# A graph network kernel: one gathered column in seven of layer 1 comes from one-hot products on TensorE

## The chip, the cores and the metric

The kernel runs on one core of a Trainium2 chip. The metric is the device time of one execution in microseconds. Five engines of the core appear in the text: TensorE (PE, with its weight loads shown apart as PEld), VectorE (DVE), ScalarE (ACT), GpSimd (POOL) and SyncE (SP). Each works through its own instructions in the order of the program and waits for others by semaphores.

## The reference

There are 12,500 nodes with 32 features and 400,000 edges `src -> dst`, sorted by `dst`. Three graph-attention layers (two of 2 heads with 16 channels, one of 1 head with 32) are followed by a residual layer norm, an edge network with a maximum over each node's edges, and a second residual layer norm. A layer is:

```python
h = (x @ W.T).reshape(n, heads, ch)
a_s = (h * att_s[None]).sum(-1); a_d = (h * att_d[None]).sum(-1)
logits = leaky_relu(a_s[src] + a_d[dst], slope)
m = segment_max(logits, dst)
ex = exp(logits - m[dst]); denom = segment_sum(ex, dst)
alpha = ex / (denom[dst] + 1e-16)
out = segment_sum(alpha[:, :, None] * h[src], dst) + bias
```

After layers 1 and 2 come an ELU and a clip to [-3, 3]. The edge network is `relu([x[src], x[dst], edge_attr] @ W1 + b1) @ W2 + b2`, of which each node takes the maximum over its edges.

## The kernel before

The sorted edges lie in 128 rows of TE = 3125, one row per partition, so that an edge column t holds one edge of each partition. The 12,500 nodes, padded to 12,544, lie as 128 partitions x NC = 98.

Preparation (up to 303 us): the node table of layer 1 (`tb`, 36 values per node: 32 features, two source logits, and the places of the node's last and first edge) is computed on TensorE and written to `table1` in DRAM. The first edge of each node is found with 98 gathers (`found`). The destination logits are scattered (`give`). `empties` fills the rows for nodes without edges in all tables, through SP's transfers.

Each of the three layers (`attention(li, idx)`) then walks over 54 chunks of the columns: 50 of T = 60, and four of 48, 32, 29 and 16. For each column one indirect DMA on POOL (`gather`, line 68) fetches 128 rows of the node table into a tile `g`; the index is `src` in layer 1, and the place of the source node's last or first edge (`src_last`, `src_first`, taken out of the gathered rows at L683 and L684) in layers 2 and 3 and in the edge network. `g` has four buffers. With a chunk's rows there, DVE and ACT work out the logits (`lg`), running maxima (`mx`) and running sums by scans along the row (`gf`, L723 multiplies, L734 scans). `finish` divides by the sums (L494 to L501), applies the ELU, and in four sub-blocks of up to 16 columns adds, transposes and multiplies with the next layer's weights (`yb` L523, `yt` L525, `ph` L528, `pa` L529, `tb` L531, `at` L532). SP writes `sums`, `table` and `give` to DRAM.

The program is recorded in source order and a scheduler then places the instructions of each engine; the work of neighbouring chunks is interleaved on DVE, PE and ACT. Each engine executes its list strictly in that order. At the end of a layer POOL scatters 49 columns of `x0` (`move`), gathers one row of `sums`, and scatters the rows of the partitions' ends, after which the next layer's gathers begin.

The edge network has the same chunks and gathers `xs` by `src_last` (four buffers). It transposes three inputs per sub-block (`xt` L870, `et` L871, `xst` L872), multiplies them with two halves of the first weights (L877) and the second weights (L883), takes the maximum by scans (L887) and normalises (`layernorm`, L540 to L548).

PSUM tiles: `small_p` is a tile of each layer's pool; the biases lie in a tile `fixed`.

Of the kernel before, what the change touches and what calls it, by code (L numbers as in the profile page):

```python
# [24 lines left out]
def gnn_resnorm_kernel(ctx: ExitStack, tc: tile.TileContext, a: dict, out: bass.AP):  # L25

# [56 lines left out]

    groups = [(c0, min(28, NC - c0)) for c0 in range(0, NC, 28)]
# [19 lines left out]
    gpool = gstack.enter_context(tc.tile_pool(name="g", bufs=4, side="right"))  # L104
# [4 lines left out]
    x0 = runs.tile([P, NC, D], F32, name="x0")  # L109
# [22 lines left out]
    fixed = ctx.enter_context(tc.tile_pool(name="fixed", bufs=1, space=PSUM)).tile([P, 512], F32, name="fixed")  # L132
    own = const.tile([P, 1], F32, name="own")
    nc.gpsimd.iota(own, pattern=[[1, 1]], base=E + NN, channel_multiplier=1,
                   allow_small_or_imprecise_dtypes=True)
    zeros = const.tile([P, 1250], F32, name="zeros")
# [59 lines left out]

    table1 = dram.tile([NN, D + 4], F32, name="table1")
# [10 lines left out]
    def clear(table, part=0, parts=1):  # L208
        flat = edge_rows(table).rearrange("p t w -> p (t w)")
        k = TE * table.shape[1] // parts  # L210
        z = next(z for z in range(1250, 0, -1) if k % z == 0)
        tc.keep_in_program_order(
            nc.sync.dma_start(out=flat[:, part * k:part * k + k].rearrange("p (k z) -> p k z", z=z),
                              in_=bcast(zeros[:, None, :z], [P, k // z, z])))
# [83 lines left out]
    cont = runs2.tile([P, TE + 1], F32, name="cont")  # L298
    src_last = runs2.tile([P, TE], I32, name="src_last")
# [14 lines left out]
    with tc.tile_pool(name="seg", bufs=1) as sp, tc.tile_pool(name="rowsp", bufs=2) as rp, \  # L314
# [52 lines left out]
        for c0, n in groups:  # L367
            rows = rp.tile([P, 28, SB], I32, name="found")
            for c in range(n):
                gather(rows[:, c, :], dst_d, find_i[:, c0 + c:c0 + c + 1])  # L370
            less = rp.tile([P, 28, SB], BF16, name="less")[:, :n, :]
            nc.vector.tensor_tensor(less, rows[:, :n, :], bcast(node_p[:, c0:c0 + n, None], [P, n, SB]), op=ALU.is_lt)
            nc.vector.tensor_reduce(r[:, c0:c0 + n], less, axis=AX.X, op=ALU.add)
            nc.vector.tensor_add(first[:, c0:c0 + n], first[:, c0:c0 + n], r[:, c0:c0 + n])
# [15 lines left out]
        nc.sync.dma_start(out=node_rows(table1), in_=tb)  # L390

# [111 lines left out]
    def finish(li, pool, psum, den, v, n, hb=1):  # L503

        y = pool.tile([P, D * T], F32, name="y")[:, :D * n].rearrange("p (f t) -> p f t", t=n)
# [11 lines left out]
        for b in range(0, n, TB):  # L517
            nt = min(TB, n - b)
            w = nt * D
            pe = psum.tile([P, TB * D], F32, name="pe")[:, :w].rearrange("p (f t) -> p f t", t=nt)  # L520
            nc.scalar.activation(pe, e[:, :, b:b + nt], AF.Identity, bias=minus[:, 1:2])  # L521
            yb = pool.tile([P, TB * D], F32, name="yb", bufs=1)[:, :w].rearrange("p (f t) -> p f t", t=nt)
            nc.vector.scalar_tensor_tensor(yb, y[:, :, b:b + nt], 3.0, pe, op0=ALU.min, op1=ALU.add)  # L523
            yt = pool.tile([P, TB * D], F32, name="yt")[:, :w]
            nc.vector.transpose(blocks(yt), yb.rearrange("p f t -> p t f"))  # L525
            ph = psum.tile([P, TB * D], F32, name="ph", bufs=hb)[:, :w]
            pa = psum.tile([P, TB * D], F32, name="pa")[:, :w]
            nc.tensor.matmul(ph, lhsT=w_bd, rhs=yt, start=True, stop=True)  # L528
            nc.tensor.matmul(pa, lhsT=a_bd, rhs=yt, start=True, stop=True)  # L529
            at = pool.tile([P, TB, D], F32, name="at")[:, :nt, :]  # L530
            nc.vector.transpose(tb[:, b:b + nt, :D], blocks(ph))  # L531
            nc.vector.transpose(at, blocks(pa))  # L532
            nc.scalar.copy(tb[:, b:b + nt, D:], at[:, :, :heads])  # L533
            nc.scalar.copy(ta[:, b:b + nt, :], at[:, :, heads:2 * heads])
        return tb, ta

    def layernorm(lp, st, x, n):
        st = st[:, :n]
        sq = lp.tile([P, T, D], F32, name="sq", bufs=1)[:, :n, :]
# [10 lines left out]
    def finish3(pool, psum, den, v, x, n):  # L550
# [4 lines left out]
        layernorm(pool, den[:, 2 * T:], x, n)  # L555

    def empties():
# [4 lines left out]
        with tc.tile_pool(name="empty", bufs=2) as ep, tc.tile_pool(name="emptyps", bufs=1, space=PSUM) as eps:  # L562
# [66 lines left out]
    def attention(li, idx):  # L629
# [10 lines left out]
        with tc.tile_pool(name=f"s{li}", bufs=2) as sp, tc.tile_pool(name=f"f{li}", bufs=2) as fp:  # L640
# [18 lines left out]
            with tc.tile_pool(name=f"ps{li}", bufs=1, space=PSUM) as psp, \  # L659
                    tc.tile_pool(name=f"fps{li}", bufs=1, space=PSUM) as fps:  # L660

                small_p = psp.tile([P, 512], F32, name="small_p")
                den = small_p[:, 128:]
                old = None
                for c, (t0, n) in enumerate(todo):
                    g = gpool.tile([P, T * (D + 4)], F32, name="g")[:, :n * w].rearrange("p (t w) -> p t w", w=w)
                    for t in range(n):
                        gather(g[:, t, :], table, idx[:, t0 + t:t0 + t + 1])
# [44 lines left out]
                    rx = psp.tile([P, heads, 512], F32, name="rx", bufs=3 - heads)  # L713
# [5 lines left out]
                    for h in range(heads):  # L719
                        nc.scalar.activation(  # L720
                            rx[:, h, :FS * (n + 1)].rearrange("p (k t) -> p k t", t=n + 1),
                            bcast(rr[:, h:h + 1, :], [P, FS, n + 1]), AF.Exp)
                        nc.vector.tensor_mul(v[:, h * wd:h * wd + ch, cur].rearrange("p f t -> p t f"),  # L723
                                             g[:, :, h * ch:(h + 1) * ch], bcast(wt[:, h, :, None], [P, n, ch]))
                        nc.scalar.copy(v[:, h * wd + ch, cur], wt[:, h, :])  # L725
# [4 lines left out]
                    for h in range(heads):  # L730
                        for f in range(0, wd, FS):
                            k = min(FS, wd - f) * (n + 1)
                            o = (h * wd + f) * (n + 1)
                            nc.vector.tensor_tensor_scan(turned(gf[:, o:o + k], rev), turned(rx[:, h, :k], rev),  # L734
                                                         turned(gf[:, o:o + k], rev), 0.0, op0=ALU.mult, op1=ALU.add)
                    rows = sp.tile([P, T, gw + heads], F32, name="rows")[:, :n, :]
# [5 lines left out]
                    if li < 3:  # L742
                        tb, ta = finish(li, fp, fps, den, v[:, :, cur], n, hb=2)
# [61 lines left out]
    def edge_network(tag, in_order):  # L805


        with tc.tile_pool(name=f"in{tag}", bufs=2) as ip, tc.tile_pool(name=f"gx{tag}", bufs=4) as gp, \
                tc.tile_pool(name=f"v{tag}", bufs=2) as vp, tc.tile_pool(name=f"t{tag}", bufs=2) as tp, \
                tc.tile_pool(name=f"pf{tag}", bufs=1, space=PSUM) as pfp, \  # L810
                tc.tile_pool(name=f"ph{tag}", bufs=1, space=PSUM) as php:
            small_p = pfp.tile([P, 512], F32, name="small_p")
# [15 lines left out]

            old = None
            loaded = load(0)  # L830
            for c, (t0, n) in enumerate(todo):
                xs = gp.tile([P, T, D], F32, name="xs")
                for t in range(n):
                    gather(xs[:, t, :], tables[4], src_last[:, t0 + t:t0 + t + 1])
# [31 lines left out]
                for b in range(0, n, TB):  # L866
                    nt = min(TB, n - b)
                    w = nt * D
                    xt, et, st = (tp.tile([P, TB * D], F32, name=x)[:, :w] for x in ("xt", "et", "xst"))
# [29 lines left out]
                layernorm(tp, small_p[:, 128:], z, n)  # L899
# [58 lines left out]
```

## Time and profile before

| | us |
|---|---|
| median of the runs (3) | 18568.16 |
| lowest and highest | 18566.3, 18571.94 |
| profiled execution | 16382.21 |
| span of the profiled execution | 16379.3 |
| layer 1: first and last gather start | 303.2, 4249.9 |
| layer 2: first and last gather start | 4317.0, 8226.8 |
| layer 3: first and last gather start | 8294.0, 12202.3 |
| busy in the span: PE, DVE, ACT, POOL | 2781.3, 6836.7, 2899.1, 12218.7 |

The profiled execution is shorter than the runs shown; all durations below are from it. A row of the profile's groups names the line, the engine, the operation and its tiles, then the count, the busy time with the mean duration in nanoseconds, and the idle time of the engine before those instructions with what ended it. A row of the order in time gives the start and the duration in microseconds. "x2" merges two records that follow each other; an fp32 matmul leaves two records.

### The profile page before, as it was taken

The page shows a single profiled execution, that of the slowest core. Times are in us where ns is not written, and L with a number is a line of the kernel's source. Part 1 is how long each engine was busy: PE and PEld are TensorE (multiplying, and loading weights), DVE is VectorE, ACT ScalarE, POOL GpSimd, SP SyncE. Part 2 cuts the span into 40 slices and gives each one's busy share as a digit, 9 for nine tenths or more (in the row PEclk, how much of TensorE's full clock was granted, in tenths as well). Part 3 has the DMA queues.
Part 4 walks back from the last instruction along what each step waited for, and adds up shares of the span by engine and source line. Part 5 has one row for each costly group of instructions (what it writes and reads, how often), then busy time and mean ns, then how long its engine had stood idle before and what let it go on. Part 6 is the DMA issues. An engine that isn't in the chain of part 4 may idle for free.

```text
span 16379.3 us, 42394 instructions
## 1 busy us (share of the span) xinstructions
PE 2781.3 (17%) x5140; PEld 1116.2 (7%) x5140; DVE 6836.7 (42%) x9700; ACT 2899.1 (18%) x3835; POOL 12218.7 (75%) x12921
## 2 busy tenths in 40 slices
PE   0111111111111111111100000000003333334342
PEld 0000000000000000000000000000001111111110
DVE  2433333333333333333333333333335666666654
ACT  0221212121212222121211111111111111111111
POOL 6777777777777777777777777777767777777775
PEclk5555555555555555555555555555556666666676
DMA  4222222222222222222222222222222222222221
GB/s 59 71 60 69 60 55 73 55 48 42 43 41 47 41 44 44 43 45 41 46 47 58 51 56 53 56 53 55 54 57 59 66 66 64 66 66 64 69 63 42
DMA packets 580809, 897.63 MB, mean 55 GB/s; under 512 B 286271, under 2 KB 490238, under 8 KB 567070
## 3 DMA queue, kind: packets, MB, share of 16 engines
q0 software_dynamic: 413088, 226.62, 12.5%
q1 hardware_dynamic: 167116, 665.01, 11.5%
q10 hardware_dynamic: 304, 3.20, 0.1%
q14 instruction: 259, 2.11, 0.0%
q8 instruction: 42, 0.69, 0.0%
HBM read 390.67 MB, written 503.27 MB: 55 GB/s over the span
## 4 chain that ended last, share of the span: by engine, by line
POOL 71%; issue 23%; DMA 3%; DVE 1%; PE 0%; ACT 0%; POOLq 0%; DVEq 0%; ACTq 0%
POOL g L68 52%; POOL xs L68 17%; DMA g<-table,src_i 1%; DMA g<-table,src_last 1%; DMA xs<-table,src_last 1%; DMA g<-table,src_first 1%; POOL give L72 1%; POOL so L68 1%; POOL x_e L72 1%; PE ph L877 0%; DMA s<-sums,at_i 0%; PE pv L883 0%; DVE vf L887 0%; DVE z L803 0%; ACT xd L889 0%
## 5 line engine op out<-in xcount | busy, mean ns | idle before, releaser
L68 POOL DMA_INDIRECT g<-table,src_i x3125 | 2958.5, 947 | 989.6 <-issue 940.2
L68 POOL DMA_INDIRECT g<-table,src_last x3125 | 2957.1, 946 | 952.7 <-issue 938.1
L68 POOL DMA_INDIRECT xs<-table,src_last x3125 | 2954.9, 946 | 955.4 <-issue 936.8
L68 POOL DMA_INDIRECT g<-table,src_first x3125 | 2955.7, 946 | 952.7 <-issue 940.8
L697 DVE TENSOR_TENSOR lg<-g,af 128x60 f32<-128x60 f32 (+4 forms) x270 | 59.3, 250 | 4422.3 <-DMA g<-table,src_first 2333.3
L528 PE MATMUL ph<-yt,w_bd 128*128 128x512 f32 (+2 forms) x840 | 669.2, 893 | 3434.1 <-DVE yt L525 3434.1
L529 PE MATMUL pa<-yt,a_bd 128*128 128x512 f32 (+2 forms) x840 | 656.7, 878 | 3307.4 <-DVE at L532 3307.0
L877 PE MATMUL ph<-xt,wb_bd 128*128 128x512 f32 (+2 forms) x832 | 466.1, 645 | 2419.0 <-DVE xt L870 2419.0
L683 DVE CAST src_last<-g 128x60 int32<-128x60 f32 (+4 forms) x54 | 12.7, 235 | 2056.4 <-DMA g<-table,src_i 2056.4
L738 ACT COPY rows<-mx 128x120 f32<-128x120 f32 (+3 forms) x162 | 49.9, 308 | 4419.8 <-DVE mx L704 4366.5
L737 ACT COPY rows<-gf 128x2040 f32<-128x2040 f32 (+3 forms) x162 | 628.4, 3879 | 648.4 <-DVE gf L734 648.4
L734 DVE TENSOR_TENSOR_SCAN gf<-rx,gf 128x488 f32<-128x488 f32 (+4 forms) x918 | 731.9, 858 | 1.4 <-ACT gf L725 0.9
L591 PE MATMUL pt<-ident,tops 128*34 128x128 f32 (+1 forms) x3 | 1.0, 322 | 3954.6 <-DVE xr L548 3952.9
L723 DVE TENSOR_TENSOR gf<-g,small_p 128x960 f32<-128x960 f32 (+5 forms) x270 | 597.8, 2214 | 63.1 <-ACT small_p L715 63.1
L523 DVE SCALAR_TENSOR_TENSOR yb<-y,pe 128x512 f32<-128x512 f32 (+2 forms) x420 | 268.7, 640 | 605.2 <-ACT pe L521 586.7
L533 ACT COPY tb<-at 128x32 f32<-128x32 f32 (+4 forms) x420 | 92.3, 220 | 2333.8 <-DVE at L532 2333.8
L528 PEld LDWEIGHTS ph<-yt,w_bd 128*128 128x128 f32 x840 | 218.6, 287 | 3845.7 <-DVE yt L525 3367.3
L879 ACT ACTIVATE ht<-ph,b_c 128x512 f32<-128x512 f32 (+2 forms) x416 | 275.1, 661 | 1144.0 <-PE ph L877 1140.2
L529 PEld LDWEIGHTS pa<-yt,a_bd 128*128 128x128 f32 x840 | 220.3, 278 | 3681.9 <-DVE at L532 3511.5
L877 PE MATMUL ph<-et,wb_bd 128*128 128x512 f32 (+2 forms) x832 | 450.1, 626 | 0.0
L877 PE MATMUL ph<-xst,wb_bd 128*128 128x512 f32 (+2 forms) x832 | 431.2, 602 | 34.3 <-DVE xst L872 34.3
L883 PE MATMUL pv<-ht,w_bd 128*128 128x512 f32 (+2 forms) x832 | 415.3, 593 | 6.1 <-DVE vf L884 2.0
(295 smaller groups left out, 8591.8 us busy)
## 6 DMA issues: line engine op xcount, KB each, us to landing
sums<-rows SPq DMA_DIRECT2D x100, 1080.0 KB, 4.2
table<-tb SPq DMA_DIRECT2D x50, 1020.0 KB, 4.1
sums<-rows SPq DMA_DIRECT2D x50, 1020.0 KB
g<-table,src_i POOLq DMA_INDIRECT x3125
x_e<-zeros SPq DMA_DIRECT2D x10, 5000.0 KB, 16.8
g<-table,src_last POOLq DMA_INDIRECT x3125
g<-table,src_first POOLq DMA_INDIRECT x3125
xs<-table,src_last POOLq DMA_INDIRECT x3125
```

What stands on the lines that cost most here:

```text
L68: return nc.gpsimd.indirect_dma_start(out=dst, out_offset=None, in_=table, in_offset=bass.IndirectOffsetOnAxis(ap=idx, axis=0))
L72: return nc.gpsimd.indirect_dma_start(out=table, in_=src, in_offset=None, out_offset=bass.IndirectOffsetOnAxis(ap=idx, axis=0))
L523: nc.vector.scalar_tensor_tensor(yb, y[:, :, b:b + nt], 3.0, pe, op0=ALU.min, op1=ALU.add)
L528: nc.tensor.matmul(ph, lhsT=w_bd, rhs=yt, start=True, stop=True)
L529: nc.tensor.matmul(pa, lhsT=a_bd, rhs=yt, start=True, stop=True)
L533: nc.scalar.copy(tb[:, b:b + nt, D:], at[:, :, :heads])
L723: nc.vector.tensor_mul(v[:, h * wd:h * wd + ch, cur].rearrange("p f t -> p t f"), g[:, :, h * ch:(h + 1) * ch], bcast(wt[:, h, :, None], [ ...
L734: nc.vector.tensor_tensor_scan(turned(gf[:, o:o + k], rev), turned(rx[:, h, :k], rev), turned(gf[:, o:o + k], rev), 0.0, op0=ALU.mult, op1 ...
L737: nc.scalar.copy(rows[:, :, :gw], v[:, :, cur].rearrange("p f t -> p t f"))
L877: nc.tensor.matmul(ph, lhsT=wb_bd[:, s, h, :], rhs=x, start=(s == 1), stop=(s == 0))
L879: nc.scalar.activation(ht, ph, AF.Relu, bias=b1_c[:, h:h + 1])
L883: nc.tensor.matmul(pv, lhsT=w2_bd[:, h, :], rhs=hts[h], start=(h == 0), stop=(h == 1))
```

## The change

In layer 1 every seventh column (t = 6, 13, 20, ...) is no longer gathered: 446 of 3125. A class `Fetch` supplies these columns from a copy of the node table that stays in SBUF. The constants are `KT, KN = 7, 14` (7 x 14 = 98 columns of nodes), and `EVERY = {1: 7, 2: 0, 3: 0, 4: 0}`, so the layers 2 and 3 and the edge network fetch nothing.

`by_group[:, k, :]` holds, for the k-th 14 node columns, 36 x 14 values per partition; seven ACT copies fill it from `tb`. A node number is split into the partition q, the group k and the column b in the group; `at = 128 k + q` and `b` are computed once for all 446 columns. For each fetched column:

- TensorE transposes and spreads `at` over the partitions (`places_p`, 128 columns);
- DVE compares it with the 7 x 128 numbers `kid`: the one-hot matrices `oh` (two buffers);
- TensorE adds seven fp32 products of a 128 x 128 one-hot matrix with 504 columns of `by_group` into one PSUM bank (`acc`, two buffers);
- DVE multiplies with the mask of `b` (`mine`) and sums over the 14 places into the column of `g`.

The rows of chunk c+1, gathered and fetched, are recorded ahead of the work on chunk c. To make room, `g` gets three buffers instead of four; `y`, `rows`, `at`, `ph`, `et`, `xst` and the tiles of `empties` get one buffer instead of two; `rx` is a tile per head; `layernorm` of the edge network writes its squares into `ea`; `small_p` and `places_p` become parts of `fixed`; `zeros` has 625 columns instead of 1250; the search for first edges works in seven groups of 14 instead of four of up to 28; `x0` lies in a pool that ends with the layers.

```diff
+    KT, KN = 7, 14
+    EVERY = {1: 7, 2: 0, 3: 0, 4: 0}
-    gpool = gstack.enter_context(tc.tile_pool(name="g", bufs=4, side="right"))
+    gpool = gstack.enter_context(tc.tile_pool(name="g", bufs=3, side="right"))
...
+    small_p, places_p = fixed[:, 128:384], fixed[:, 384:]
+    kid = const.tile([P, KT], F32, name="kid")
+    nc.gpsimd.iota(kid, pattern=[[P, KT]], base=0, channel_multiplier=1, allow_small_or_imprecise_dtypes=True)
-    zeros = const.tile([P, 1250], F32, name="zeros")
+    zeros = const.tile([P, 625], F32, name="zeros")
...
+    def group(k, rows, w):
+        nc.scalar.copy(by_group[:, k, :KN * w].rearrange("p (w b) -> p w b", b=KN), rows.rearrange("p b w -> p w b"))
+    class Fetch:
+        def __init__(self, stack, name, every, w):
...
+                nc.vector.tensor_copy(node, src_i[:, :m * every].rearrange("p (i c) -> p i c", c=every)[:, :, every - 1])
+                divide(q, r, node, NC, q_i, k)
+                divide(k, self.b, r, KN, q_i, node)
+                nc.vector.scalar_tensor_tensor(self.at, k, float(P), q, op0=ALU.mult, op1=ALU.add)
...
+        def fetch(self, psum, g, t0, n, bufs=2):
+            todo = [t for t in range(t0, t0 + n) if t in self]
...
+            bm = pool.tile([P, 9, KN], F32, name="bm")[:, :len(todo), :]
+            nc.vector.tensor_tensor(bm, bcast(count[:, None, :KN], [P, len(todo), KN]),
+                                    bcast(self.b[:, i0:i0 + len(todo), None], [P, len(todo), KN]), op=ALU.is_equal)
+            def ones_of(m):
+                nc.tensor.matmul(places_p, lhsT=bcast(self.at[:, i0 + m:i0 + m + 1], [P, P]), rhs=ident,
+                                 start=True, stop=True)
+                oh = pool.tile([P, KT, P], F32, name="oh")
+                nc.vector.tensor_tensor(oh, bcast(places_p[:, None, :], [P, KT, P]),
+                                        bcast(kid[:, :, None], [P, KT, P]), op=ALU.is_equal)
+                return oh
+            coming = ones_of(0)
+            for m, t in enumerate(todo):
+                oh = coming
+                if m + 1 < len(todo):
+                    coming = ones_of(m + 1)
+                acc = psum.tile([P, 512], F32, name="acc", bufs=bufs)[:, :KN * w]
+                for k in range(KT):
+                    nc.tensor.matmul(acc, lhsT=oh[:, k, :], rhs=by_group[:, k, :KN * w],
+                                     start=(k == 0), stop=(k == KT - 1))
+                mine = pool.tile([P, D + 4, KN], F32, name="mine")[:, :w, :]
+                nc.vector.tensor_mul(mine, acc.rearrange("p (w b) -> p w b", b=KN),
+                                     bcast(bm[:, m:m + 1, :], [P, w, KN]))
+                nc.vector.tensor_reduce(g[:, t - t0, :w], mine, axis=AX.X, op=ALU.add)
...
-        for c0, n in groups:
-            rows = rp.tile([P, 28, SB], I32, name="found")
+        for c0, n in ((k * KN, KN) for k in range(KT)):
+            rows = rp.tile([P, KN, SB], I32, name="found")
...
         nc.sync.dma_start(out=node_rows(table1), in_=tb)
+        for k in range(KT):
+            group(k, tb[:, k * KN:(k + 1) * KN, :], D + 4)
...
-        with tc.tile_pool(name="empty", bufs=2) as ep, tc.tile_pool(name="emptyps", bufs=1, space=PSUM) as eps:
+        with tc.tile_pool(name="empty", bufs=1) as ep, tc.tile_pool(name="emptyps", bufs=1, space=PSUM) as eps:
...
+                def rows_of(c):
+                    t0, n = todo[c]
+                    g = gpool.tile([P, T * (D + 4)], F32, name="g")[:, :n * w].rearrange("p (t w) -> p t w", w=w)
+                    for t in range(n):
+                        if t0 + t not in fetch:
+                            gather(g[:, t, :], table, idx[:, t0 + t:t0 + t + 1])
+                    fetch.fetch(psp, g, t0, n)
+                    return g
                 old = None
+                coming = rows_of(0)
                 for c, (t0, n) in enumerate(todo):
-                    g = gpool.tile([P, T * (D + 4)], F32, name="g")[:, :n * w].rearrange("p (t w) -> p t w", w=w)
-                    for t in range(n):
-                        gather(g[:, t, :], table, idx[:, t0 + t:t0 + t + 1])
+                    g = coming
+                    if c + 1 < len(todo):
+                        coming = rows_of(c + 1)
...
-                    xt, et, st = (tp.tile([P, TB * D], F32, name=x)[:, :w] for x in ("xt", "et", "xst"))
+                    xt, et, st = (tp.tile([P, TB * D], F32, name=x, bufs=k)[:, :w]
+                                  for x, k in (("xt", 2), ("et", 1), ("xst", 1)))
```

## The prediction

> **What bounds the kernel now.** I read four views in this order: the page's busy line and chain, its cost groups, the stages, and the order of time inside one chunk.
>
> ```profile
> span 16379.3 us, 42394 instructions
> PE 2781.3 (17%) x5140; PEld 1116.2 (7%) x5140; DVE 6836.7 (42%) x9700; ACT 2899.1 (18%) x3835; POOL 12218.7 (75%) x12921
> POOL 71%; issue 23%; DMA 3%; DVE 1%; PE 0%; ACT 0%; POOLq 0%; DVEq 0%; ACTq 0%
> L68 POOL DMA_INDIRECT g<-table,src_i x3125 | 2958.5, 947 | 989.6 <-issue 940.2
> ```
>
> The chain is POOL and POOL's own issue time: 94% of the span. A gather takes 0.947 us and 0.30 us pass before the next: 1.25 us each, 75.0 us for a chunk of 60, and nothing else is on the path.
>
> The stages (length, then busy PE, PEld, DVE, ACT, POOL, granted PE clock, DMA share): one row inside layer 1, one inside the edge network.
>
> ```profile
> 2000.00:3000.00 1000.00, 165.48 (x215) 57.23 (x213) 382.32 (x652) 212.41 (x299) 756.42 (x800) 0.57 0.26 62
> 13000.00:14000.00 1000.00, 389.81 (x860) 168.87 (x861) 613.92 (x667) 186.40 (x226) 756.12 (x801) 0.68 0.24 66
> ```
>
> POOL issues 800 gathers per 1000 us in both, though DVE is 38% busy in one and 61% in the other: a busier DVE does not slow a gather. In layer 1 DVE has 28.7 us of work per chunk.
>
> The longest waits of DVE in a chunk, in order of time around 2068:
>
> ```profile
> 2068.96 0.21 DVE L683 CAST src_last<-g 128x60 int32<-128x60 f32 x1 [38.40 <-DMA g<-table,src_i]
> ```
>
> DVE sits 38 us per chunk at `src_last`, for the chunk's last gather. That is the room into which the change puts its work.
>
> **What is removed.** 446 of 3125 layer-1 gathers (one column in seven, 3125//7): 446 x 1.25 = 558 us of POOL. A chunk has 60/7 = 8.57 fetched columns and 51.43 gathers, so POOL needs 64.3 us for it instead of 75.0.
>
> **What is added, per fetched column.** TensorE: one 128-column matmul (`places_p`) and seven fp32 matmuls of 504 columns. DVE: `oh` (896 elements), `mine` (504), a reduction of 504. The nearest rows:
>
> ```profile
> 13543.60 0.30 PEld L883 LDWEIGHTS pv<-ht,w_bd 128*128 128x128 f32 x2 [0.75 <-ACT ht L879]
> 13544.56 1.02 PE L877 MATMUL ph<-xt,wb_bd 128*128 128x512 f32 x2
> 13545.42 1.02 PE L877 MATMUL ph<-et,wb_bd 128*128 128x512 f32 x2
> 13546.28 1.02 PE L877 MATMUL ph<-xst,wb_bd 128*128 128x512 f32 x2
> 312.99 1.04 DVE L570 TENSOR_TENSOR z<-x,fixed 128x896 f32<-128x896 f32 x1
> 440.15 0.63 DVE L544 TENSOR_REDUCE sm<-sq 128x14 f32<-128x448 f32 x1 [0.70 <-ACT sq L543]
> ```
>
> From start to start an fp32 matmul of 512 columns, with new weights each time, takes 0.86 us; of 504, 0.845; seven are 5.9 us. With 0.4 us for the 128-column one (the edge of rows like `pt<-ident,x`, 0.34 each record) a column costs PE 6.3 us. DVE: 1.05 for `oh` (same size, one operand in PSUM), 0.68 for `mine` (`yb`, 512 elements, 688 ns), 0.70 for the reduction: 2.4 us. Per chunk that is 54 us of PE and 21 us of DVE. DVE ends at 50 us of 75 and is no bound by itself; PE ends at 54 + 7 (the two projections of `finish`, eight matmuls) = 61 us, just under POOL's 64.3.
>
> [...]The seven matmuls could also run at half clock:
>
> ```profile
> 13535.42 2.07 PE L877 MATMUL ph<-xt,wb_bd 128*128 128x512 f32 x2 [46.06 <-DVE xt L870]
> 13537.28 1.92 PE L877 MATMUL ph<-et,wb_bd 128*128 128x512 f32 x2
> 13538.99 1.26 PE L877 MATMUL ph<-xst,wb_bd 128*128 128x512 f32 x2
> ```
>
> After 46 us of idle the first two come 1.86 and 1.71 us apart, the third 1.1, then 0.86. [...] But the edge network also has groups of four to six with 0.75 us waits between (the `LDWEIGHTS` row above) and stays at 0.86. I take the row, and one half-clock start per chunk (2.4 us).
>
> **The ring of DVE and PE.** Both engines work in order, so the chunk's period is the longer of POOL's and a ring through the new instruction order. I walked it with the durations above. (a) From the end of the third-last column of chunk c+1: DVE does `mine`, `oh`, reduce (2.4), then chunk c's `gf`, scans, denominators and `y` with two more columns between: 1.93 + 2.35 + 1.93 + 2.35 + 1.4 + 2.25 + 2.15 + 2 x 1.4 + `oh` 1.05 = 18.2; together 20.6. PE has only two columns for that time (12.6) and then stands still for 8 us, because the single `places_p` is held until `oh` has read it. (b) Column 0 restarts cold: 6.3 + 2.4 = 8.7. (c) Column 1 is interleaved with the eight matmuls of `finish` and their transposes: 13.6. (d) The remaining n-4 columns: 6.3 each. Sum 42.9 + 6.3(n-4): 68.1 for n = 8, 74.4 for 9, mean 71.7. This counts no small waits. On the same links the stage's DVE rows show 23.1 us (`at<-pa`) and 7.7 us (`tb<-ph`) of waiting in 13.3 chunks, 2.3 us per chunk; with 1 us for the new links the ring is **75 us**. Bounds: 69 (half the places cost, no waits) and 84 (one wait of about 1 us at every column).
>
> So the waiting of POOL's 64.3 us would be hidden under a ring of 75: off the path, POOL stops at the three `g` buffers.
>
> **Edges and the rest.** `empties` now has single buffers, so each of its four groups waits for the transfer of the one before; the transfers queue behind two slow table fills (SP's queue is held until 396 us). Then come 20 DVE operations on 446 elements (about 12 us) and the whole of chunk 0's columns (8 x 6.3). `src_last` of chunk 0 moves from 416.6 to about 500: +84 us, between 0 (POOL had caught up anyway) and 120. At the end of layer 1 POOL's 49 `move` scatters (62 us, 4250 to 4313), which cover the tail now, are done early: -15. Seven ACT copies into `by_group` (1 us each) and the `kid` iota lie under the same table fills. SP issues the same transfers; clearing pieces of 625 instead of 1250 elements double the descriptors of eleven transfers at a DMA share of a quarter: 0. Layers 2 and 3 lose a buffer of `g`, `y`, `ph`, `at`, `rows`; the cover is DVE's 38 us wait; without it a serial `finish` would cost some 5 us per chunk. In the edge network `et` and `xst` are single: each is refilled while PE does the second half's last product and `pv` (2.6 us against 0.7 each): 0.
>
> **From the profile to the runs.** The profiled execution took 16382.2 us (span and 2.9). The runs shown have a median of 18568.16: 2186 us more. Since POOL's chain is 94%, and other engines would have to double to matter, I read this as POOL's cadence: 2186/12921 = 0.17 us more per instruction, 1.42 per gather, 85.1 us per chunk. By the profile's own cadence the sum is 52.08 chunks x (75 - 75.0) + 84 - 15 = +69: 16,450. By the runs' cadence POOL needs 51.43 x 1.42 = 73.0, the ring 75: 52.08 x (75 - 85.1) = -526, + 84: **-442, 18,126**.
>
> **Rivals.**
> - *A (forecast), 0.56*: runs' POOL slower, other engines as profiled: 18,130; own range 17,940 (ring under 73: 446 x 1.42 = 633 saved) to 18,450. For: no other engine carries 2186 us.
> - *B, 0.27*: the 2186 us are one pause, or all engines are slower alike. Then the ring only replaces POOL's wait: 18,568 + 70 = 18,640, from 18,470 (ring 71.7) to 18,760. Against: three runs agree within 6 us.
> - *C, slower, 0.16*: the fetch runs at half clock. Place: the seven matmuls, after every wait for `oh`. Price: 5.9 us per column, 307 us over 52 chunks. It decides from a ring of 83.5, that is from 1.5 of 8.57 columns cold; all cold gives 118 us per chunk: 18,568 + 1,713 + 84 = 20,370. Against: the edge rows above.
> - *D, 0.01*: the gathers are not removed. The program lists 446 `oh`, `mine` and reductions, so hardly.
>
> **Numbers.** 18,130; range 17,940 to 18,740 (A and B and the mildest C). A difference under 0.2% (37 us) cannot be told from none. Faster: 0.55 of A + 0.09 of B = 0.64; same 0.05; slower 0.16 (C) + 0.15 (B and A's end) = 0.31.
>
> **What would show it.** Right: 2679 layer-1 gathers; `src_last` of chunk 0 near 500; in layer 1 POOL idle about 10 us per chunk, released by DVE; `src_last` no longer waiting 38 us; PE busy about 80% with seven matmuls in 5.9 us; one PE gap of about 8 us per chunk before `places_p`; a profiled span near 16,450 while the median falls. Wrong: matmuls of `acc` 1.7 us apart (C); chunk periods of 64 us (the ring is shorter than I walked); gathers of another duration; any change in the period of layers 2, 3 or the edge network.

## Result and the profile after

The changed kernel takes **20,488.6 us** (median of four runs, 20,486.6 to 20,492.9) where the kernel before takes 18,570.1 (18,566.3 to 18,575.6): a ratio of **1.103, 95% interval 1.101 to 1.105**. The prediction said 18,130, between 17,940 and 18,740, so it is wrong in sign and far outside its range.

The kernel before takes about 18,550 us on some chips and 16,352 on another, and its first profile (16,382) was of the second sort, while its runs, and those of the change above, were of the first; below, every time is compared with the kernel before on the same chip.

The page of the changed kernel (span and busy engines; chain; then groups with busy time, mean ns and the idle time before them by releaser):

```profile
span 20491.1 us, 58374 instructions
...
PE 5989.2 (29%) x12276; PEld 2540.4 (12%) x12276; DVE 7905.0 (39%) x11121; ACT 2900.5 (14%) x3842; POOL 12500.2 (61%) x12476
...
POOL 33%; issue 17%; another core or an unknown queue 16%; PE 15%; DVE 15%; ACT 4%; DMA 0%; DVEq 0%; POOLq 0%; SPq 0%; ACTq 0%
...
L70 POOL DMA_INDIRECT g<-table,src_i x2679 | 2532.5, 945 | 3410.2 <-DVE gf L824 2574.5
L70 POOL DMA_INDIRECT xs<-table,src_last x3125 | 2971.6, 951 | 1958.8 <-DVE xst L983 1013.2
L70 POOL DMA_INDIRECT g<-table,src_last x3125 | 3298.9, 1056 | 1055.4 <-issue 1044.2
```

The gathers were removed as planned (2679 left in layer 1, 945 ns each), and POOL now stands 2,575 us waiting for `gf`, that is for a free `g` buffer. The chain has a part that the first profile of before did not have: 16% "another core or an unknown queue", time in which an engine waits for a signal whose sender the profile cannot name (`<-remote` in the rows; an unnamed wait below). Only one core runs, so these are signals that came long after the work that sent them, as the rows below show.

The stage rows, one stretch in layer 1 and one in the edge network (busy PE, PEld, DVE, ACT, POOL, granted clock, DMA share):

```profile
2000.00:3000.00 1000.00, 596.58 (x1315) 261.23 (x1314) 419.62 (x660) 139.37 (x198) 437.18 (x463) 0.76 0.17 40
16000.00:17000.00 1000.00, 364.34 (x698) 150.20 (x697) 473.39 (x520) 146.71 (x179) 591.66 (x628) 0.66 0.18 50
```

In layer 1 POOL issues 463 gathers per 1000 us and no engine is busy over 60%. From one `src_last` to the next it is 109.6 us (eight columns) or 117.1 (nine): 113.9 on average over chunks 4 to 45, where the ring was walked to 75.

The stretch in which the time goes: the two engines inside part (c), column 1 interleaved with `finish` (start us, busy us, engine, line; in brackets the idle time before it).

```profile
2368.27 1.02 PE L611 MATMUL ph<-yt,w_bd 128*128 128x512 f32 x2
...
2369.13 1.02 PE L612 MATMUL pa<-yt,a_bd 128*128 128x512 f32 x2
...
2369.99 1.01 PE L260 MATMUL acc<-by_group,oh 128*128 128x504 f32 x2
...
2374.06 0.68 DVE L263 TENSOR_TENSOR mine<-acc,bm 128x504 f32<-128x504 f32 x1 [8.75 <-remote]
...
2390.17 0.72 DVE L614 STREAM_TRANSPOSE tb<-ph 128x512 f32<-128x512 f32 x1 [14.24 <-remote]
...
2391.95 2.05 PE L611 MATMUL ph<-yt,w_bd 128*128 128x512 f32 x2 [20.95 <-issue]
...
2396.46 0.72 DVE L615 STREAM_TRANSPOSE at<-pa 128x512 f32<-128x512 f32 x1 [4.66 <-remote]
...
2407.66 0.72 DVE L614 STREAM_TRANSPOSE tb<-ph 128x512 f32<-128x512 f32 x1 [9.91 <-remote]
```

The first `ph` was written at 2369.3 and DVE may read it only at 2390.2; `pa` was written at 2370.2 and is read at 2396.5. TensorE is idle for 21 us meanwhile, since the next `ph` needs the single buffer. The trace's own record of TensorE's semaphore shows the same: the five matmuls that raise it end at 2367.4, 2367.6, 2368.4, 2369.3 and 2370.2, and its steps come at 2374.0, 2379.7, 2385.2, 2390.2 and 2396.4, one per 5 to 6 us. This record has gaps elsewhere, but the three DVE instructions that wait start 0.02 us behind a step. During this stretch POOL's gathers start every 1.25 us. Some 45 us later, when POOL has run out of `g` buffers, the backlog goes at once and DVE again starts right behind TensorE.

Where the 1,965 us lie, by stages (profile of after against the second profile of before, run e1 below; the ends of the stages are first and last gathers and `src_last`): the start of layer 1, +179 (`src_last` of chunk 0 at 593.1 instead of 414.2); its other chunks, +1,489; the step to layer 2, -79 (33.0 us instead of 112.0, as the scatters are done early); layers 2 and 3, +6 and 0; the edge network, +382 (4,926.7 instead of 4,544.8); the rest -12.

### The profile page after: what moved, and what is told of

Same layout as the page of the kernel before. It is cut to its first block, busy times and chain, and to the rows that moved or that the text cites. A ratio compares the mean times of both kernels' runs of the same rounds, so it can differ in the third digit from the quotient of the medians.

```text
span 20491.1 us, 58374 instructions
## 1 busy us (share of the span) xinstructions
PE 5989.2 (29%) x12276; PEld 2540.4 (12%) x12276; DVE 7905.0 (39%) x11121; ACT 2900.5 (14%) x3842; POOL 12500.2 (61%) x12476
## 4 chain that ended last, share of the span: by engine, by line
POOL 33%; issue 17%; another core or an unknown queue 16%; PE 15%; DVE 15%; ACT 4%; DMA 0%; DVEq 0%; POOLq 0%; SPq 0%; ACTq 0%
POOL g L70 31%; PE acc L260 7%; PE ph L988 4%; PE pv L994 2%; DVE gf L830 1%; DVE xf L974 1%; DVE vf L998 1%; DVE gf L824 1%; ACT xd L1000 1%; DVE xf L964 1%; DVE z L899 1%; DVE yt L608 1%; ACT ht L990 1%; DVE y L580 1%
## 5 line engine op out<-in xcount | busy, mean ns | idle before, releaser
L70 POOL DMA_INDIRECT g<-table,src_i x2679 | 2532.5, 945 | 3410.2 <-DVE gf L824 2574.5
L70 POOL DMA_INDIRECT g<-table,src_last x3125 | 3298.9, 1056 | 1055.4 <-issue 1044.2
L70 POOL DMA_INDIRECT g<-table,src_first x3125 | 3301.2, 1056 | 1047.0 <-issue 1032.0
L260 PE MATMUL acc<-by_group,oh 128*128 128x504 f32 x6244 | 2955.9, 624 | 2.7 <-DVE oh L249 2.7
L260 PEld LDWEIGHTS acc<-by_group,oh 128*128 128x128 f32 x6244 | 1252.7, 206 | 1427.4 <-issue 1410.1
L994 PE MATMUL pv<-ht,w_bd 128*128 128x512 f32 (+2 forms) x832 | 528.5, 725 | 1149.3 <-ACT ht L990 952.0
L263 DVE TENSOR_TENSOR mine<-acc,bm 128x504 f32<-128x504 f32 x446 | 303.6, 681 | 1408.0 <-PE acc L260 922.4
L614 DVE STREAM_TRANSPOSE tb<-ph 128x512 f32<-128x512 f32 (+2 forms) x420 | 282.7, 673 | 1413.9 <-remote 1025.5
L824 DVE TENSOR_TENSOR gf<-g,fixed 128x960 f32<-128x960 f32 (+5 forms) x270 | 602.0, 2230 | 65.4 <-issue 63.7
L981 DVE STREAM_TRANSPOSE xt<-xf 128x512 f32<-128x512 f32 x208 | 218.8, 1071 | 975.7 <-remote 675.0
```

Of the source, the lines that this page charges most:

```text
L70: return nc.gpsimd.indirect_dma_start(out=dst, out_offset=None, in_=table, in_offset=bass.IndirectOffsetOnAxis(ap=idx, axis=0))
L260: nc.tensor.matmul(acc, lhsT=oh[:, k, :], rhs=by_group[:, k, :KN * w], start=(k == 0), stop=(k == KT - 1))
L263: nc.vector.tensor_mul(mine, acc.rearrange("p (w b) -> p w b", b=KN), bcast(bm[:, m:m + 1, :], [P, w, KN]))
L994: nc.tensor.matmul(pv, lhsT=w2_bd[:, h, :], rhs=hts[h], start=(h == 0), stop=(h == 1))
```

## Experiments

**e1, the kernel before with a second profile.** No edit.

> The kernel before, unchanged, with a second profile. Two theories for the 2,190 us between its first profile (16,382) and its runs (18,570). Signals theory (S): in the ordinary state of this program the signals that TensorE sends to other engines arrive late while gathers land (in the kernel after one of them per 5.6 us, in part c of the ring). Then this profile is close to 18,570, DVE rows such as tb<-ph and at<-pa wait several us for a matmul that ended long before, and the gathers of layers 2 and 3 take about 1.06 us with 1.39 us from one to the next, as in the kernel after. Change theory (C): the late signals come with the fetch. Then this profile is again near 16,380, or 18,570 with nothing but longer gathers, and DVE waits for TensorE under 1 us.

Measured: 18,530.0 us beside 18,532.6. Its page:

```profile
span 18526.6 us, 42394 instructions
...
POOL 55%; issue 21%; DVE 9%; another core or an unknown queue 7%; PE 6%; ACT 2%; DMA 1%; DVEq 0%; POOLq 0%; ACTq 0%
...
L68 POOL DMA_INDIRECT xs<-table,src_last x3125 | 2978.5, 953 | 1570.1 <-issue 943.5
L68 POOL DMA_INDIRECT g<-table,src_i x3125 | 3298.9, 1056 | 1070.0 <-issue 1046.5
```

and, from DVE's groups of 2000 to 3000 us,

```profile
L531 DVE STREAM_TRANSPOSE tb<-ph 128x512 f32<-128x512 f32 (+1 forms) x47 | 31.5, 670 | 5.7 <-PE ph L528 4.3 <-issue 1.4
```

Same program, same instruction count, but slower throughout. A gather of layer 1 takes 1.056 us on average with 0.34 before the next: 1.40 us from one to the next instead of 1.25, and nearly the same in layers 2 and 3; 83.5 us per chunk of layer 1. The guess of 1.42 was good. The 1.40 is a mean: half of the gathers between 2000 and 3000 us still follow within 1.30 us, and one in ten takes over 1.54. The unnamed waits are here too (7% of the chain; the longest group is ACT's `ht` behind `ph`, 1,020 us, in the edge network, where POOL's gathers take 0.953 us and follow every 1.25 while it issues), but in layer 1 DVE waits for `ph` and `pa` hardly at all. So theory S is half right: the late signals do not come with the change alone, but in layer 1 of before they do not appear.

**e2, all of the change but the fetch.**

```
-    EVERY = {1: 7, 2: 0, 3: 0, 4: 0}
+    EVERY = {1: 0, 2: 0, 3: 0, 4: 0}
```

> All of the change but the fetch itself: EVERY is 0 in layer 1, so all 3125 columns are gathered; the single buffers, the shared PSUM bank, rows one chunk ahead and by_group stay. If the fetch costs the time (S or any theory of the ring): 18,500 to 18,700, layer 1 near 85 us per chunk. If the lost buffers or the shared bank cost it (B): 20,000 or more, layers 2, 3 and the edge network as slow as in the kernel after.

Measured: 18,871.2 us, ratio 1.018 (1.015 to 1.021). Layer 1 ends at 4,679 as in before (4,676); layers 2 and 3 are unchanged; the edge network takes 4,909. So it takes the fetch to make layer 1 long, and something else of the change costs the edge network some 360 us. B holds for that one stage only.

**e3, one column in fourteen.** `EVERY = {1: 14, ...}`.

> One column in fourteen instead of one in seven, 4.3 per chunk. If the loss is per column (each column's links or its products, theory P): half of 1,920, so 19,500, layer 1 near 97 us per chunk. If it is the part of the ring where column 1 is interleaved with finish (S: some nine signals of TensorE, 5.6 us each, while gathers land), that part stays at about 50 us and only columns at 6.1 to 7.5 us go: 110 - 4.3 x 7 = 80 us, then POOL's 55.7 gathers at 1.4 us = 78 are nearly as long: 18,400 to 18,900.

Measured: 19,396.4 us, ratio 1.047, 93.4 us per chunk. The number lies by theory P (half the excess), but the view does not: with half of the columns, the 42 reads of `ph` in a stretch of 1000 us wait 336 us, more than in the kernel after (247 us for 36). The loss is not per column. Neither theory gave this number.

**e4, one of the seven products.** It leaves out six sevenths of the fetched nodes.

```
-                for k in range(KT):
-                    nc.tensor.matmul(acc, lhsT=oh[:, k, :], rhs=by_group[:, k, :KN * w],
-                                     start=(k == 0), stop=(k == KT - 1))
+                nc.tensor.matmul(acc, lhsT=oh[:, 0, :], rhs=by_group[:, 0, :KN * w],
+                                 start=True, stop=True)
```

> Of the seven products of a fetched column only the first is made (it leaves out six sevenths of the fetched nodes); oh, mine, the reduction and all links stay. If the load of TensorE's instructions makes its signals late (theory I): the waits of 14 us at tb<-ph go, layer 1 falls to POOL's 73 us per chunk, 18,000. If it is the signals beside gathers (S): the columns get shorter by 5 us each (about 35 us per chunk), but tb<-ph still waits over 5 us with its matmul long done: 75 to 85 us per chunk, 18,100 to 18,700.

Measured: 18,957.7 us, ratio 1.023, 84.8 us per chunk (of TensorE's work 8.57 x 6 x 0.845 = 43 us per chunk are gone). DVE's groups, 2000 to 3000 us:

```profile
L613 DVE STREAM_TRANSPOSE tb<-ph 128x512 f32<-128x512 f32 (+1 forms) x47 | 32.1, 684 | 162.4 <-remote 59.0 <-PE pa L611 38.6 <-PE acc L259 38.4
L614 DVE STREAM_TRANSPOSE at<-pa 128x512 f32<-128x512 f32 (+1 forms) x46 | 31.0, 674 | 130.0 <-remote 115.8 <-issue 14.2
```

With TensorE's products nearly gone, the waits for its signals stay (292 us per 1000, 175 of them unnamed). Not the amount of its work makes them late; theory I falls.

**e5, no gathers in layer 1** (it leaves out all of them; one plain POOL transfer of neighbouring rows per run of six columns):

```
-                        if t0 + t not in fetch:
+                        if t0 + t not in fetch and (li > 1 or (t0 + t) % 7 < 0):
                             gather(g[:, t, :], table, idx[:, t0 + t:t0 + t + 1])
+                    t = 0
+                    while li == 1 and t < n:
+                        k = (t0 + t) % 7
+                        m = min(6 - k, n - t)
+                        if k >= 0 and m > 0:
+                            nc.gpsimd.dma_start(out=g[:, t:t + m, :],
+                                                in_=node_rows(table)[:, (t0 + t) % 91:(t0 + t) % 91 + m, :])
+                        t += max(m, 1) if k >= 0 else 1
```

> Leaves out all gathers of layer 1: the six neighbouring columns between two fetched ones are filled by one plain POOL transfer with rows of other nodes (8.6 transfers per chunk in place of 51.4 gathers); the fetch, TensorE's and DVE's work and order are as in the kernel after. If TensorE's signals are late only while gathers land (contention, K): the pure ring of DVE and TensorE shows, 72 to 80 us per chunk as walked in the prediction, the 14 us wait of tb<-ph gone, 20,490 - 54 x 35 = 18,600. If the ring is long by its own links (order, single buffers, the shared bank; L): POOL was not on its path, so 110 to 114 us per chunk stay, 20,300 to 20,500.

**e6, half of the gathers** (e5 with `< 3` and `>= 3`: three of each six are left out), **e7, two buffers for `et` and `xst`** (`("et", 1), ("xst", 1)` becomes `("et", 2), ("xst", 2)`) and **e8, `small_p` out of the shared PSUM bank**:

```
-    small_p, places_p = fixed[:, 128:384], fixed[:, 384:]
+    small_p, places_p = const.tile([P, 256], F32, name="small_s"), fixed[:, 384:]
```

> As the kernel after, but three of each six gathered columns of layer 1 are filled by one plain POOL transfer with rows of other nodes (this leaves out half of the gathers: 25.7 gathers and 8.6 transfers per chunk). POOL's work per chunk then lasts some 40 us instead of 64. K: the late signals last only while gathers land, so part c (53 us from the start of finish) shortens to 25 to 35 us: 90 to 95 us per chunk, 19,400 to 19,700. L: no change, 113 us per chunk.

> The kernel after with two buffers again for et and xst in the edge network. The edge network took 4,545 us in the second profile of before and 4,927 in that of after. If the single buffers cost the 382 us: 20,110. If it is the rows gathered one chunk ahead, or something else of the change: 20,490.

> The kernel after with small_p in SBUF, so that places_p no longer shares a PSUM bank with ACT's exponentials and DVE's denominators; the order on TensorE changes with it: two of the eight projections of finish come before column 0's products. If the shared bank's waits make the ring long (part a, 8 us of TensorE idle, and ACT waiting some 29 us per chunk behind oh): 90 to 100 us per chunk, 19,500. K: part a gets shorter by up to 8 us, but the late signals stay: 103 to 112 us per chunk, 19,950 to 20,450.

These four fell on the chip where before takes 16,352.3 us, for which none of the expectations was written. Measured: e5 16,148.2, e6 16,158.4, e7 16,165.7, e8 16,642.3 us. e7's stage row, and from its groups of 2000 to 3000 us DVE's reads of `ph`:

```profile
2000.00:3000.00 1000.00, 891.99 (x2189) 411.31 (x2189) 669.89 (x1055) 216.88 (x308) 692.98 (x734) 0.94 0.25 61
```

```profile
L614 DVE STREAM_TRANSPOSE tb<-ph 128x512 f32<-128x512 f32 (+1 forms) x56 | 38.0, 678 | 19.9 <-PE ph L611 17.5
```

Here nothing waits for an unnamed sender: 56 reads of `ph` wait 19.9 us, all named. The ring takes 66.0 to 73.5 us per chunk, 70.2 on average, with all gathers (e7), half (e6: 70) or none (e5: 70), so on this chip POOL is off the path and the ring of DVE and TensorE is the bound, as walked. e7 is 1.1% faster than before (16,165.7/16,352.3, one run each), and e5's edge network, with single `et` and `xst`, takes the same 3,900 us as e7's with two. The change itself was not run on this chip; its layer 1 is e7's and its edge network e5's, so an estimate from these is about 16,165 there. For the theories of the 10% these runs decide nothing. What e8 did is told at the end.

**e9, gathers paced**; **e10, after again**; **e11, e5 again**; **e12, e7 again**, all beside a before of 18,533.8. The edit of e9:

```
                             gather(g[:, t, :], table, idx[:, t0 + t:t0 + t + 1])
+                            if li == 1:
+                                tc.keep_in_program_order(nc.gpsimd.memset(pace, 0.0))
...
+    pace = const.tile([P, 128], F32, name="pace")
```

> The kernel after with one POOL memset (128x128, 0.205 us in the first profile) behind each gather of layer 1, so that the gathers come about 1.45 us apart instead of 1.25; TensorE's order is unchanged. Where the kernel before takes about 18,550 (every gather there comes 1.40 us apart on average and nothing is gained by issuing faster): if gathers issued faster than that crowd out TensorE's signals (K), pacing them frees the signals and the ring falls from 113 to 75 to 85 us per chunk, 18,500 to 19,000. If the ring is long by itself (L), or the signals are late beside gathers at any pace: 20,400 to 20,600. Where the kernel before takes about 16,350: POOL needs 74.6 us per chunk, so 16,300 to 16,450.

> The kernel after, unchanged, beside the kernel before on the same chip. The kernel before took 18,530 to 18,570 in some calls and 16,352 in another, where three relatives of the kernel after took 16,150 to 16,170 and no DVE row waited without a visible releaser. If that goes with the chip: on one with 18,550 for before, after takes 20,490; on one with 16,350, it takes 16,160 to 16,250, with 66 to 73.5 us per chunk in layer 1. If it goes with the single buffers et and xst (which one of those relatives did not have): 20,490 on both.

> Leaves out all gathers of layer 1 as in the earlier run of this edit, where the ring took 69.9 us per chunk beside a before of 16,352, the same as with its gathers. If before takes about 18,550 here: contention (K) says the ring is again about 70 us, as no gather lands in layer 1, so 20,490 - 54 x 43 = 18,150; a chip that is slower in TensorE's signals at all times (M) gives 100 us and more per chunk, 20,000 to 20,400. If before takes 16,350: 16,150 again.

> The kernel after with two buffers again for et and xst in the edge network. If before takes about 18,550 here: 20,110 if the single buffers cost the 382 us that the edge network lost in the profile of after, 20,490 if they do not (the rows recorded one chunk ahead, or more late signals). If before takes 16,350: 16,166 again.

Measured, one run each: e10 20,456.3, as in the runs above. e11 18,255.8: the ring is 70.2 us, to a tenth of a microsecond that of the other chip. DVE's groups from 2000 to 3000 us, first of after and then of e11:

```profile
L263 DVE TENSOR_TENSOR mine<-acc,bm 128x504 f32<-128x504 f32 x73 | 49.7, 681 | 229.9 <-PE acc L260 145.2 <-remote 74.4 <-issue 10.3
...
L614 DVE STREAM_TRANSPOSE tb<-ph 128x512 f32<-128x512 f32 (+1 forms) x36 | 24.6, 684 | 247.0 <-remote 203.8 <-issue 28.5 <-PE ph L611 10.2
L615 DVE STREAM_TRANSPOSE at<-pa 128x512 f32<-128x512 f32 (+1 forms) x36 | 24.2, 673 | 84.3 <-remote 83.3
```

```profile
L263 DVE TENSOR_TENSOR mine<-acc,bm 128x504 f32<-128x504 f32 x123 | 83.8, 681 | 280.2 <-PE acc L260 280.2
...
L614 DVE STREAM_TRANSPOSE tb<-ph 128x512 f32<-128x512 f32 (+1 forms) x56 | 38.0, 679 | 19.9 <-PE ph L611 17.5
L615 DVE STREAM_TRANSPOSE at<-pa 128x512 f32<-128x512 f32 (+1 forms) x56 | 36.5, 651 | 1.6
```

The order on TensorE and DVE is the same, and the 51.4 gathers of a chunk have given way to 8.6 plain transfers: the unnamed waits (74 + 204 + 83 us per 1000; e10, on e11's chip, has 53 + 217 + 83) are gone with them. K is shown, L and M fall: TensorE's signals are late beside gathers, and nothing else makes this ring longer than walked.

e12 took 20,100.1 us, 356 less than e10; its edge network is back at 4,547 us, and POOL's row reads as in e1:

```profile
L70 POOL DMA_INDIRECT xs<-table,src_last x3125 | 2978.4, 953 | 1572.6 <-issue 944.0
```

So on this chip the single `et` and `xst` cost what the edge network lost, though they cost nothing on the other: by this reading, a wait for a buffer that is short when signals are prompt.

e9 took 19,786.3 us, 100.2 per chunk, between the two theories. The memset (0.221 us) fills part of the 0.30 us between gathers, so they came 1.34 us apart and not 1.45, still below the 1.40 that this chip keeps on average in layers 2 and 3; the unnamed waits of DVE fell from 361 to 203 us per 1000. The experiment had not reached the point that it was to test.

**e13 and e14, slower paces**: e9 with the tile at 256 and 384 columns, and two buffers for `et` and `xst`. **e15**: one column in fourteen with 192 columns, and the same buffers.

> The paced kernel with a memset of 128x256 behind each gather of layer 1 (0.306 us in the first profile; the 128x128 one brought the gathers from 1.25 to 1.34 us apart, so this one to about 1.43), and two buffers again for et and xst. Beside a before of 18,530: 51.4 gathers x 1.43 = 73.5 us per chunk. If a pace slower than the 1.40 us that the gathers of layers 2 and 3 keep there sets TensorE's signals free (K): 74 to 80 us per chunk, 18,250 - 356 + 54 x 6 = 18,200 to 18,500, faster than before. If the pace only thins the late signals in proportion: 1.25 gave 114, 1.34 gave 100, so 1.43 gives 86: 18,750. If the paced kernel's gain came from something else than the pace: 19,430 (e9 less 356). Beside a before of 16,350: POOL's 73.5 us, 16,300 to 16,400.

> As the kernel with the 128x256 memset, but 128x384: gathers about 1.53 us apart, POOL 78.7 us per chunk. Beside a before of 18,530: K: 79 to 82 us per chunk, 18,400 to 18,550, POOL the bound; in proportion: the ring falls to 72 and POOL's 79 remain, the same. A ring of 90 and more would say that signals are late beside gathers at any pace. Beside a before of 16,350: 16,600.

> One column in fourteen, a memset of 128x192 behind each gather of layer 1 (about 1.385 us apart, 55.7 gathers, 77 us per chunk), two buffers for et and xst. TensorE sends half as many signals for the fetch. Beside a before of 18,530: unpaced, one in fourteen took 93.8 us per chunk. K: 77 to 83 us per chunk, 18,300 to 18,550. If pace does not matter here: 94 us per chunk, 19,050. Beside a before of 16,350: 16,500.

Measured, beside a before of 18,535.5: e13 **18,051.7 us, ratio 0.974 (0.971 to 0.977)**; e14 18,316.5, ratio 0.988 (0.985 to 0.991); e15 18,432.4, ratio 0.994 (0.992 to 0.996). The same groups of e13, with POOL's two:

```profile
L264 DVE TENSOR_TENSOR mine<-acc,bm 128x504 f32<-128x504 f32 x115 | 77.9, 677 | 243.6 <-PE acc L261 235.7 <-issue 7.9
...
L615 DVE STREAM_TRANSPOSE tb<-ph 128x512 f32<-128x512 f32 (+1 forms) x56 | 37.9, 677 | 23.6 <-PE ph L612 21.1 <-PE acc L261 1.2
L616 DVE STREAM_TRANSPOSE at<-pa 128x512 f32<-128x512 f32 (+1 forms) x56 | 36.6, 654 | 1.9
...
L70 POOL DMA_INDIRECT g<-table,src_i x691 | 660.8, 956 | 114.8 <-issue 114.8
L759 POOL MEMSET pace<- 128x256 f32 x690 | 226.6, 328 | 0.4
```

691 gathers start in this stretch and none of these waits is unnamed. The same rows of e15:

```profile
L264 DVE TENSOR_TENSOR mine<-acc,bm 128x504 f32<-128x504 f32 x54 | 36.8, 681 | 259.9 <-remote 233.6 <-PE acc L261 13.7 <-PE fixed L247 8.1
...
L615 DVE STREAM_TRANSPOSE tb<-ph 128x512 f32<-128x512 f32 (+1 forms) x49 | 33.3, 680 | 177.7 <-remote 86.7 <-PE acc L261 67.7 <-issue 10.0
...
L70 POOL DMA_INDIRECT g<-table,src_i x691 | 658.3, 953 | 147.7 <-issue 114.6 <-DVE gf L827 33.1
```

By pace (start to start, median of 2000 to 3000 us), chunk of layer 1 (mean of chunks 4 to 45) and unnamed waits of DVE from 2000 to 3000 us, on chips where before takes 18,550:

| kernel | a gather every | layer 1, us per chunk | POOL's need, gathers x pace | unnamed waits of DVE, us |
|---|---|---|---|---|
| after | 1.25 us | 113.9 | 64.3 | 361 |
| e9 | 1.34 | 100.2 | 68.9 | 203 |
| e13 | 1.44 | 72.6 | 74.1 | 0 |
| e14 | 1.55 | 78.1 | 79.7 | 0 |
| e11 | none | 70.2 | - | 0 |
| e15, one column in fourteen | 1.39 | 80.6 | 77.3 | 376 |

(The means of e13 and e14 lie below POOL's need because the first 20 and 10 chunks run at the ring's 70 while POOL still has full `g` buffers ahead.) Up to 1.39 us the ring stretches; from 1.44 on it is its own 70 and POOL is the bound. It is the pace and not the presence of gathers: slowing POOL, which was off the path, by 0.19 us per gather takes 41 us off every chunk. e15's number lies in the range that its expectation gave to K, but not for K's reason: at 1.39 us its signals are as late as in the kernel after, its chunks take 42 to 117 us, and POOL again waits for `gf`. It starts 691 gathers in the same 1000 us as e13, so what counts is the pace inside a burst and not the number per 1000 us.

e13 beats both kernels where before takes 18,550; where it takes 16,352 it was not run, and POOL's 74 us per chunk against the 75 of before would leave it, by estimate, within a per cent of before.

## Why the prediction was wrong

**Right, on either chip.** The gathers left, 2679. A fetched column on TensorE: 6.14 us from one to the next (6.3 said), 0.85 per product, as said from the edge rows (the granted clock of e7's stage is 0.94, and 1.00 in four whole columns of after, 4476.5 to 4500.5 us), so the price taken from those rows held; DVE 1.08 + 0.68 + 0.67 = 2.43 (2.4). POOL stops at the `g` buffers. Layers 2 and 3 unchanged. The order in the ring and its parts (a), (b) and (d) as walked: one TensorE gap before `places_p` (6.3 us, 8 said), 8.6 us for the restart (4411.0 to 4419.6, with a granted clock of 0.50 up to 4414; 8.7 said). Without late signals the whole ring is 70.2 (71.7 walked, 75 with waits).

**Right in size, wrong in what was made of it.** From the first profile to the runs: 2,186 us over POOL's instructions gave 1.42 us per gather and 85.1 per chunk; measured 1.40 and 83.5. But the step "other engines would have to double to matter" took all else over from the first profile. What made POOL slower in the runs did not only slow POOL. Before, POOL was the bound, its gathers came 1.40 us apart on average, and in layer 1 TensorE's few signals came through. After, POOL has slack and issues each burst at 1.25 us, and the time is lost on TensorE's signals, which are on the path. Why it falls on the gathers in one kernel and on the signals in the other is not shown.

**The term that failed**: part (c) of the ring, 13.6 us, measured 56.6 (TensorE from column 1's first product at 4419.6 to its end at 4476.2, in a chunk from the middle). There `mine` and the first two pairs of `tb<-ph` and `at<-pa` wait 8.75, 14.24, 4.66, 9.91 and 4.05 us (chunk at 2358) for TensorE's signals in the middle of POOL's burst: 41.6 us, where the walk allowed 3.3 for all waits of a chunk (2.3 taken from the first profile, 1 for the new links). The 43 us by which part (c) is long are nearly all of the 44 by which the ring is (113.9 against 70.2). 52 x (113.9 - 83.5) = 1,581 us took the place of -526.

**The small terms.** The start of chunk 0: +84 said, with 120 as the end; +179 measured here and 503 - 417 = 86 on the other chip (e7). Tail of layer 1: -15 said (and left out of the sum for the runs), -79 measured. Clearing in pieces of 625: 21,760 packets of 2,500 bytes instead of 10,880 of 5,000, the doubling that was said. The copies into `by_group`: 1.07 us each (1 said). Edge network: 0 said, +382 here (e12 shows the buffers), 0 there (e5).

**Rivals.** C named the right place, the fetch, and by chance the right size (118 us per chunk, its estimate at 5.9 us more per column), but by the clock: products 1.7 us apart, where in whole columns they came 0.85 apart. The half clock itself is in the traces: 0.50 granted from 13535 to 13539 us of before, the cold rows of the prediction, and 1.00 from 13541 to 13546; in after 0.50 from 4445 to 4448 and from 4450 to 4455 us, where TensorE stops in part (c). B (the ring only takes the place of POOL's wait) has the sign and not the price. None had a signal that is late after its work is done; the first profile showed none, and a wait's price was taken from it for runs that it did not describe. The warning stood in the text: the profile was 12% under the runs, and that gap was filled with one number for one engine.

## What to carry to other kernels

When a profile and the runs differ by much more than the runs among themselves, get a profile that agrees with the runs before costing a change; the resource that explains the gap may also price the new work. An engine freed from the critical path runs ahead in bursts, and others may pay for them: slowing it to a pace that can be sustained (here 1.44 us per gather instead of 1.25) took the kernel with two `et` and `xst` buffers from 20,100 (e12) to 18,052 us (e13), so that with the buffers a 10% loss became a 2.6% gain. Single buffers that cost nothing with prompt signals cost 360 us with late ones.

## What the hardware showed unexpectedly

- The same program takes 18,530 to 18,575 or 16,352 us, with gathers 1.40 or 1.25 us apart on average, and the sign of this change goes with it (+10%, and about -1% by e5 and e7). The slow kind was met on chips 15 (e1 to e4, e13 to e15) and 4 (e9 to e12), the fast on chip 1 (e5 to e8) alone, so that it is the chip, and not the occasion, is likely and not shown.
- Where gathers come every 1.25 to 1.39 us there, TensorE's signals are late (one per 5 to 6 us in the stretch shown). What holds them is open. The record of the DMA semaphores' events goes with it: from 2000 to 2500 us the first profile of before has 6,389 for its 399 gathers, 16 for each, and e1 has 527 where that rate gives some 5,728; of the events of all DMAs, at 16 for each (6,837 for 427 in the first profile of before), after has 815 of 4,080, e9 1,030 of 4,432 and e15 1,258 of 5,968, but e13, on e15's chip, has 5,113 of 5,968, and e11 all. So where nearly all events are on record no signal is late, though in e1's layer 1, where most are missing, it is the gathers that are slow and TensorE's few signals that are not. Whether the missing events and the late signals have one cause is not shown. Every run of the experiments has a recorded span and clock; whether signals are late, and the change a loss, in an execution that is not recorded is not shown.
- e8 (before 16,352.3): with `small_p` in SBUF layer 1 ended 255 us earlier than e7's, but all later stages got slower, as some gathers now take 2 to 4 us. Rows of POOL and of DVE in layer 3:

```profile
9146.39 3.77 DVE L824 TENSOR_TENSOR gf<-g,small_s 128x1920 f32<-128x1920 f32 x1 [1.30 <-ACT small_s L811]
...
9146.88 3.95 POOL L70 DMA_INDIRECT g<-table,src_first  x1 [0.30 <-issue]
...
9155.58 2.17 DVE L580 TENSOR_TENSOR y<-gf,small_s 128x1920 f32<-128x1920 f32 x1
9156.13 2.41 POOL L70 DMA_INDIRECT g<-table,src_first  x1 [0.30 <-issue]
```

  The gather begun beside `gf` ends 0.7 us after it (9150.83 against 9150.16); with the operand in PSUM (e7) the longest gather from 9000 to 10000 us takes 0.970. From 9140 to 9260 us eight gathers of e8 take over 1.5 us (1.99 to 3.95), and all eight begin while DVE runs an instruction that reads `small_s` and another SBUF tile, and end 0.67 to 0.82 us after it; all 614 indirect transfers of e8 over 1.5 us overlap such an instruction. What holds them is not shown. The place of that small operand, chosen for a free bank, was worth 255 us in one stage and cost some 730 in the others.
